# A graph layer on one core: GpSimd's order in the table stage, the last norm's square root and the width of the last down products

## The chip, the cores and the metric

The kernel runs on one core of one Trainium2 chip. The metric is the device time of one launch in microseconds (us); the time of a kernel is the median of its runs. The parts of the core are called PE (TensorE, the matmuls; PEld are its weight loads), DVE (VectorE), ACT (ScalarE), POOL (GpSimd) and SP (SyncE, which here only issues DMAs).

## The reference

625 nodes with 512 features, 20,625 edges sorted by destination (each with a source, one of four types and a weight). The layer is a normalized graph convolution, a feed-forward part and two more norms:

```python
h = relu(layernorm(x))
for r in range(4):
    msg += (h[src] @ W_rel[r] + b_rel[r]) * where(edge_type == r, edge_weight, 0)[:, None]
agg = segment_sum(msg, dst) / max(segment_sum(edge_weight, dst), 1)[:, None]
x1 = layernorm(h + h @ W_self + b_self + agg) * ln1_g + ln1_b
ffn = gelu(x1 @ W_ffn1 + b_ffn1) @ W_ffn2 + b_ffn2
out = x + layernorm(x1 + ffn) * ln2_g + ln2_b
```

W_rel and W_self are 512x512, W_ffn1 is 512x1024, W_ffn2 1024x512. All is float32.

## The kernel before, in words

The nodes lie in five blocks of 128 rows (the last has 113), the edges in 162 tiles of 128.

**Table stage** (lines 511 to 565, to about 116 us). For each of the four types r and each block i, `table_rows` (L218) multiplies the block of h by W_rel[r], adds the bias row and stores the 128x512 result into a table in DRAM, 20 blocks in all. In the first round each block's h must be made first: `variance` (L164) takes mean and variance on DVE, `pre_norm` (L207) takes 1/sqrt on POOL as a power of -0.5 (`rsqrt_pow`, L188), forms the bias nb on DVE (L210) and applies norm and relu on ACT (L211); `transposed` (L196) turns the block on PE and copies it with ACT into hT (L201). The turn of block i + 1 is written between the two halves of block i's four products (`between`, L221), and `next_norm(i + 2)` behind it. PE also adds up the edges of the first and last node block by one-hot products (`outer_hots`, `outer_sums`), which take key columns from `outer_columns` (L297).

`set_limits` (L258) fills `lim`, two rows of 162 numbers on each partition, by one POOL memset for each stretch of equal values (66 for the lower limits, 65 for the upper). The call for the lower ones is written after `next_norm(1)`, that for the upper ones at the end of the first round of r. The lower ones are read in `outer_columns` (L307), and both in `count_outside` (L268).

The order on an engine is the order written in the program for the engines that are named in `manual_schedule` (L511: PE, DVE, ACT). POOL isn't named, and there a scheduler chooses the order: all 131 memsets stand between the power of block 0 and that of block 1. SP issues the loads, the stores of the table and the later weights in order; the first twelve loads wait for nothing, later weights are issued between table stores.

**Edge stage** (L568 on). Tiles of edges are gathered from the table by indirect DMAs on POOL (L579), weighted on ACT and DVE and added up on PE by one-hot matmuls. A planner with written costs (`offer`, `run`, L616 on) puts the other work of PE between them: self products, products of the outer blocks, and for each block that is complete `norm_and_feed` (L631).

**The tail of a block**: `first_norm` (L449), a turn, and `feed_forward` (L461): eight steps `up` (four 128x128 products each, then a gelu on ACT into gT) and four steps `down` (two 128x512 products each). The last `down` step goes on: it adds the residual (L481), takes the statistics (L482), subtracts the mean and multiplies by g2 (L484, `ya`), takes 1/sqrt and forms the output (L486), and `store_block` (L491) issues the store. For four of the blocks 1/sqrt is made on DVE by `rsqrt_scaled` (L176: a shift and an integer step for the first guess, then three Newton steps of two operations, the result scaled by -8192; g1 and g2 are divided by that beforehand). The last block to be fed (`last`, L633) uses `rsqrt_pow` on POOL, a power and a multiplication, in both norms.

Behind this stands a branch (L696) that isn't taken with these inputs.

Of the kernel before, what the change touches and what calls it, by code (L numbers as in the profile page):

```python
# [9 lines left out]
F32 = mybir.dt.float32  # L10
F32R = mybir.dt.float32r
I32 = mybir.dt.int32
BF16 = mybir.dt.bfloat16
AF = mybir.ActivationFunctionType
ALU = mybir.AluOpType

P = 128
# [25 lines left out]
def gnn_layer(ctx, tc, x, edges, w_self, w_rel, w_ffn1, w_ffn2, rows_in, bf1_in, out, n_edges):  # L43
# [27 lines left out]
    HOTS = 4  # L71
# [92 lines left out]
    def variance(in_, name):  # L164

        st = work.tile([P, 6], F32, tag="bn", name=f"st_{name}")
        nc.vector.bn_stats(st, in_)
        mv = work.tile([P, 2], F32, tag="mv", name=f"mv_{name}", bufs=HOTS)
        nc.vector.bn_aggr(mv, st)
        t = work.tile([P, 3], F32, tag="rs", name=f"rs_{name}", bufs=HOTS)  # L170
        nc.vector.tensor_scalar(t[:, 0:1], mv[:, 1:2], EPS, None, op0=ALU.add)
        return mv[:, 0:1], t
# [124 lines left out]
    def outer_columns():  # L297


        ki = early.tile([P, 2, NE], I32, name="ki")  # L300
        nc.vector.tensor_copy(fl, ed[:, 0:3, :])
        k = 0
        for b, j0, n in outer:
            to, at = slice(k, k + n), slice(j0, j0 + n)
            nc.vector.tensor_scalar(ki[:, 0, to], ed[:, 0, at], P - 1, None, op0=ALU.bitwise_and)
            nc.vector.tensor_scalar(ki[:, 1, to], ed[:, 0, at], 7, None, op0=ALU.logical_shift_right)
            nc.vector.tensor_scalar(key[:, 2, to], lim[:, 0, at], float(b * P), None, op0=ALU.max)  # L307
            nc.vector.tensor_sub(key[:, 2, to], dst_f[:, at], key[:, 2, to])
            nc.vector.tensor_copy(w2[:, 0, to], wgt[:, at])
            nc.vector.tensor_sub(w2[:, 1, to], wgt[:, at], w2[:, 0, to].bitcast(F32))  # L310
            k += n
        nc.vector.tensor_copy(key[:, 0:2, :], ki)
        k = 0
        for _, j0, n in outer:
            to, at = slice(k, k + n), slice(j0, j0 + n)
            nc.vector.scalar_tensor_tensor(key[:, 1, to], typ_f[:, at], float(NB), key[:, 1, to],
                                           op0=ALU.mult, op1=ALU.add)
            k += n
        nc.vector.scalar_tensor_tensor(key[:, 1, :], key[:, 2, :], float(NC), key[:, 1, :],
                                       op0=ALU.mult, op1=ALU.add)  # L320
# [137 lines left out]
        return x1  # L458


    def feed_forward(x1T_b, gT, zi, xi, store, name, pool_pow=False, nn=P):  # L461
        po = []

        def up(f):
            pu = ps.tile([P, D], F32, tag="ps", name=f"pu_{name}_{f}")
            for k in range(KD):
                nc.tensor.matmul(pu[:, :nn], w1_sb[:, k, f * P:(f + 1) * P], x1T_b[:, k, :nn],  # L467
                                 start=(k == 0), stop=(k == KD - 1))
            nc.scalar.activation(gT[:, f, :nn], pu[:, :nn], AF.Gelu, bias=bf1[:, f:f + 1])

        def down(f):
            if f == 0:
                po.append(ps.tile([P, D], F32, tag="ps", name=f"po_{name}"))
            for f_ in (f, f + 1):
                nc.tensor.matmul(po[0][:nn], gT[:, f_, :nn], w2_sb[:, f_, :], start=(f_ == 0), stop=(f_ == KF - 1))  # L475
            if f + 2 < KF:
                return
            y = work.tile([P, D], F32, tag="ow", name=f"y_{name}", bufs=HOTS)
            if nn < P:
                nc.vector.tensor_copy(y, zi)  # L480
            nc.vector.tensor_add(y[:nn], po[0][:nn], zi[:nn])  # L481
            mean, t = variance(y, f"y{name}")  # L482
            a = work.tile([P, D], F32, tag="ow", name=f"ya_{name}", bufs=HOTS)
            nc.vector.scalar_tensor_tensor(a, y, mean, g2_bc, op0=ALU.subtract, op1=ALU.mult)  # L484
            rstd = rsqrt_pow(t, True) if pool_pow else rsqrt_scaled(t)
            nc.vector.scalar_tensor_tensor(y, a, rstd, xi, op0=ALU.mult, op1=ALU.add)  # L486
            store(y)

        return [lambda f=f: up(f) for f in range(KF)] + [lambda f=f: down(f) for f in range(0, KF, 2)]

    def store_block(b, o):  # L491
        n = min(P, N - b * P)
        whole = n if n == P else n // 16 * 16
        nc.sync.dma_start(out[b * P:b * P + whole, :], o[:whole])
        if whole < n:
            nc.scalar.dma_start(out[b * P + whole:N, :], o[whole:n])


    DG = 27
# [8 lines left out]
    for _, _, n in outer:  # L508
        groups += [(k + a, min(2, n - a)) for a in range(0, n, 2)]
        k += n  # L510
    with tc.manual_schedule(engines={PE, DVE, ACT}):  # L511
        stats = variance(xs[:, 0, :], "x0")

        def next_norm(i):
            nonlocal stats
            if i < NB:
                pre_norm(i, *stats)
            if i + 1 < NB:
                stats = variance(xs[:, i + 1, :], f"x{i + 1}")

        warm = ps_one.tile([P, D], F32, tag="one", name="warm")
        for _ in range(WARM):
            nc.tensor.matmul(warm, zeros[:, :P], zeros, start=True, stop=True)
        next_norm(0)
        hots, hots_1, made = [], [], 0
        pdeg = ps_one.tile([P, D], F32, tag="one", name="pdeg")
        transposed(hT, z[:, 0, :], 0, "h0")
        next_norm(1)
        set_limits(0)
        for r in range(R):  # L530
            for i in range(NB):
                def next_transposed():
                    transposed(hT, z[:, i + 1, :], i + 1, f"h{i + 1}")
                    next_norm(i + 2)

                table_rows(r, i, next_transposed if r == 0 and i + 1 < NB else None)
                while hots_1:
                    outer_sums(*hots_1.pop(0))
                if (r, i) == (0, 2):
                    outer_columns()  # L540
                for _ in range(2):
                    if (r, i) >= (0, 2) and groups:
                        hots_1.append(outer_hots(*groups.pop(0)))
                if (r, i) == (0, NB - 1):
                    set_limits(1)
                if (r, i) == (1, 0):
                    nc.scalar.activation(gelu_of, ones, AF.Gelu)
                    edge_columns()
                    cols = degree_columns()
                if r == 1:  # L550
                    nc.vector.tensor_add(z[:, i, :], z[:, i, :], bself_bc)
                    nc.vector.tensor_add(xs[:, i, :], xs[:, i, :], b2_bc)
                if (r, i) == (2, 0):
                    for g_bc in (g1_bc, g2_bc):
                        nc.vector.tensor_scalar(g_bc, g_bc, 1.0 / RS, None, op0=ALU.mult)
                if len(hots) > HOTS - 1 and (r, i) > (3, 0):
                    degree_sums(pdeg, *hots.pop(0))
                if r >= 2 and i > 0 and made < len(chunks):
                    hots.append(degree_hots(*chunks[made], *cols))
                    made += 1  # L560
                if (r, i) == (1, NB - 1):
                    total_outside = count_outside()
            later_loads(r)
        for made_ in hots_1:
            outer_sums(*made_)
    early_stack.close()
    edge = ctx.enter_context(tc.tile_pool(name="edge", bufs=3))
    with tc.manual_schedule(engines={PE}):  # L568
# [62 lines left out]
        def norm_and_feed(b):  # L631
            nonlocal ready
            last = b == inner[-1]  # L633
            need_self(b)
            x1 = first_norm(z[:, b, :], acc[b], rdeg[:, b:b + 1], b, pool_pow=last)
            ready = max(ready, now + NORM)
            ff = feed_forward(x1T[:, :, b * P:(b + 1) * P], gT, z[:, b, :], xs[:, b, :],
                              lambda o: store_block(b, o), b, pool_pow=last, nn=min(P, N - b * P))
            work_ = [(0.9, 1.0 if f == KF - 1 else 0.0, st) for f, st in enumerate(ff[:KF])]
            work_ += [(1.72, 0.0, st) for st in ff[KF:]]  # L640
            work_.append((0.0, 0.0, feed_next))

            def turned():
                transposed(x1T, x1, b, f"x1_{b}")
                to_feed.append(work_)
                if len(to_feed) == 1:
                    offer(10, now + 1.9, work_)

            offer(9, now + (9.0 if last else 15.0), [(0.7, 0.0, turned)])
# [46 lines left out]
    with tc.If(ends["outside"] > 0):  # L696
# [26 lines left out]
        with tc.For_i(0, NB, 1) as b:  # L723
# [11 lines left out]
            transposed(x1T, x1, 0, "x1_again")  # L735
            gT = const.tile([P, KF, P], F32, tag="gT", name="gT_again")
            for step in feed_forward(x1T[:, :, :P], gT, zb, xb,
                                     lambda o: nc.sync.dma_start(out[bass.ds(b * NG, NG), :], o[:NG]), "again"):
                step()


# [39 lines left out]
```

## Time and profile before

| | us |
|---|---|
| three runs | 322.49, 322.87, 326.82 |
| median | 322.87 |
| profiled execution, its time | 321.32 |
| its span | 319.6 |
| PE busy | 297.4 (93%) |
| DVE busy | 223.4 (70%) |
| ACT busy | 148.6 (46%) |
| POOL busy | 121.8 (38%) |

The span is what lies between the first and the last record of the execution; the rest of its time lies around it. Most of POOL's busy time (110.0 us) is the issue of 105 indirect DMAs. In the timeline a line gives the start, the duration, the engine, the line of the program, the operation and its tiles, and in brackets how long the engine was idle before, and what ended that. In the waits, a line gives who waited for whom, the sum, the number of times and the longest. DMA lines give the issuing queue, how many, the size of one, and the median time from issue to landing in us.

### The profile page before, as it was taken

Reading aid. Unit: us, or ns where it says so; the run is one execution under the profiler, and the core shown is the slowest. Engines: PE = TensorE matmul, PEld = TensorE weight load, DVE = VectorE, ACT = ScalarE, POOL = GpSimd, SP = SyncE. Lnnn points to the kernel's source line nnn. Section 1 sums busy time; section 2 is a strip of 40 time slices with the busy share of each in tenths; the row PEclk is TensorE's granted clock in tenths of the full one; section 3 lists DMA queues with packets and bytes.
Section 4 is the critical chain, followed back from the end, with each engine's and each line's share of the span. In section 5 each row is a group of like instructions: output and inputs, shape, how many; then the busy total and the mean of one; then the engine's idle time right before and its main releaser. Section 6 shows DMA issues by size and latency. Waiting matters only on the chain.

```text
span 319.6 us, 4430 instructions
## 1 busy us (share of the span) xinstructions
PE 297.4 (93%) x1360; PEld 187.5 (59%) x1361; DVE 223.4 (70%) x499; ACT 148.6 (46%) x313; POOL 121.8 (38%) x257
## 2 busy tenths in 40 slices
PE   7799999999999999999999999989999999999900
PEld 3344656665656675455456546865885975958500
DVE  3535698769999854666667999676999786965030
ACT  3236666455445634454465303676564655613100
POOL 7400000000000027777777703777774777310010
PEclk9999999999999999999999999999999999999985
DMA  7999911510011137868888823677773777500000
GB/s 242 369 403 386 371 47 66 165 66 33 34 68 51 49 106 224 261 183 256 299 297 284 252 77 101 175 215 203 206 208 115 199 204 205 151 29 33 5 35 0
DMA packets 20557, 53.33 MB, mean 167 GB/s; under 512 B 2817, under 2 KB 2817, under 8 KB 20402
## 3 DMA queue, kind: packets, MB, share of 16 engines
q0 software_dynamic: 8400, 27.53, 29.3%
q1 hardware_dynamic: 12128, 25.47, 21.9%
q8 instruction: 12, 0.20, 0.2%
q14 instruction: 15, 0.12, 0.1%
q10 hardware_dynamic: 2, 0.00, 0.0%
HBM read 45.16 MB, written 7.83 MB: 166 GB/s over the span
## 4 chain that ended last, share of the span: by engine, by line
PE 81%; DMA 4%; DVE 4%; POOL 3%; issue 3%; ACT 2%; POOLq 0%; ACTq 0%
PE pt L223 20%; PE po L475 11%; PE pu L467 9%; PE acc L441 9%; PE bank L357 8%; PE acc L603 7%; PE acc L602 7%; PE pz L238 5%; DMA ms<-table,row_i 3%; PE pdeg L402 2%; POOL lim L262 1%; POOL ms L579 1%; DVE lo L586 1%; DMA xs<-in_x_dram 1%; ACT ohw L334 1%
## 5 line engine op out<-in xcount | busy, mean ns | idle before, releaser
L579 POOL DMA_INDIRECT ms<-table,row_i x105 | 110.0, 1047 | 149.0 <-ACT sums_w L362 101.6
L584 ACT ACTIVATE hi<-ms,ed 128x512 fp32r<-128x512 f32 x105 | 74.8, 722 | 76.9 <-DMA ms<-table,row_i 37.0
L586 DVE SCALAR_TENSOR_TENSOR lo<-ms,ed,hi 128x512 fp32r<-128x512 f32 x105 | 77.8, 748 | 34.3 <-ACT hi L584 29.7
L223 PE MATMUL pt<-wr,hT 128*128 128x512 f32 x160 | 73.1, 598 | 0.8 <-ACT hT L201 0.7
L602 PE MATMUL acc<-hi,oh 128*128 128x512 f32 x117 | 61.4, 525 | 0.0
L334 ACT ACTIVATE ohw<-os,w 128x128 fp32r<-128x128 f32 x138 | 42.2, 389 | 23.5 <-DVE os L328 23.5
L603 PE MATMUL acc<-lo,oh 128*128 128x512 f32 x117 | 47.0, 402 | 1.5 <-DVE lo L586 1.4
L223 PEld LDWEIGHTS pt<-wr,hT 128*128 128x128 f32 x160 | 28.9, 190 | 29.6 <-issue 28.2
L467 PEld LDWEIGHTS pu<-x1T,w_sb 128*128 128x128 f32 x320 | 40.3, 191 | 3.3 <-ACT x1T L201 1.1
L467 PE MATMUL pu<-x1T,w_sb 128*128 128x128 f32 (+1 forms) x320 | 40.8, 275 | 0.7 <-ACT x1T L201 0.7
L357 PE MATMUL bank<-od,ohw 128*128 128x60 f32 (+18 forms) x216 | 40.0, 326 | 0.4 <-ACT ohw L334 0.4
L357 PEld LDWEIGHTS bank<-od,ohw 128*128 128x128 f32 x216 | 31.2, 191 | 10.8 <-issue 4.6
L475 PE MATMUL po<-w_sb,gT 128*128 128x512 f32 (+1 forms) x80 | 36.6, 592 | 0.0
L603 PEld LDWEIGHTS acc<-lo,oh 128*128 128x128 f32 x117 | 22.1, 189 | 14.4 <-DVE lo L586 6.4
L230 DVE TENSOR_TENSOR m<-pt,brel_bc 128x512 f32<-128x512 f32 x20 | 13.8, 688 | 21.5 <-PE pt L223 21.5
L441 PE MATMUL acc<-tr,sums_w 128*128 128x512 f32 x60 | 28.0, 595 | 0.3 <-DMA tr<-table 0.2
L602 PEld LDWEIGHTS acc<-hi,oh 128*128 128x128 f32 x117 | 22.2, 189 | 10.4 <-issue 5.5
L337 DVE TENSOR_SCALAR od<-key_row,key 128x320 fp32r<-128x320 f32 (+15 forms) x69 | 22.9, 374 | 0.0
L475 PEld LDWEIGHTS po<-w_sb,gT 128*128 128x128 f32 (+1 forms) x80 | 14.8, 187 | 13.6 <-issue 12.1
L598 DVE TENSOR_TENSOR oh<-fl,node_row 128x512 fp32r<-128x512 f32 (+1 forms) x30 | 19.9, 674 | 1.6 <-PE bank L357 1.6
L362 ACT COPY sums_w<-bank 128x500 f32<-128x500 f32 (+1 forms) x12 | 10.6, 919 | 20.3 <-PE bank L357 20.3
L238 PE MATMUL pz<-ws_sb,hT 128*128 128x512 f32 x40 | 17.6, 595 | 0.0
(107 smaller groups left out, 215.2 us busy)
## 6 DMA issues: line engine op xcount, KB each, us to landing
table<-m SPq DMA_DIRECT2D x20, 256.0 KB, 2.0
w_sb<-in_L_gnn_W_ffn_dram SPq DMA_DIRECT2D x2, 2048.0 KB, 10.6
tr<-table SPq DMA_DIRECT2D x15, 256.0 KB, 4.0
wr<-in_L_gnn_W_rel_dram SPq DMA_DIRECT2D x3, 1024.0 KB, 7.8
ms<-table,row_i POOLq DMA_INDIRECT x105, 3.8
rows<-in_rows_dram SPq DMA_DIRECT2D x1, 1536.0 KB, 14.8
z_kept<-z SPq DMA_DIRECT2D x5, 256.0 KB, 2.0
ws_sb<-in_L_gnn_W_self_dram SPq DMA_DIRECT2D x1, 1024.0 KB, 9.5
```

The costliest lines, as they stand in the source:

```text
L223: nc.tensor.matmul(p, hT[:, k, i * P:(i + 1) * P], wr_sb[r][:, k, :], start=(k == 0), stop=(k == KD - 1))
L238: nc.tensor.matmul(p, hT[:, k, i * P:(i + 1) * P], ws_sb[:, k, :], start=(k == 0), stop=(k == KD - 1))
L334: nc.scalar.activation(ohw[:, k - k0, part, :], oh[:, k - k0, :], AF.Copy, scale=w2[:, part, k:k + 1].bitcast(F32))
L357: nc.tensor.matmul(bank[q][:, (a - q * BW) * NC:(z_ - q * BW) * NC], ohw[:, k - k0, part, :], ow[:, (a - lo) * NC:(z_ - lo) * NC], start=F ...
L441: nc.tensor.matmul(acc[b], sums_w[b][:, order[i], :], kept[order[i]], start=(i == 0), stop=(i == NC - 1))
L467: nc.tensor.matmul(pu[:, :nn], w1_sb[:, k, f * P:(f + 1) * P], x1T_b[:, k, :nn], start=(k == 0), stop=(k == KD - 1))
L475: nc.tensor.matmul(po[0][:nn], gT[:, f_, :nn], w2_sb[:, f_, :], start=(f_ == 0), stop=(f_ == KF - 1))
L579: nc.gpsimd.indirect_dma_start(out=ms, out_offset=None, in_=table[:, :], in_offset=bass.IndirectOffsetOnAxis(ap=row_i[:, j:j + 1], axis=0))
L584: nc.scalar.activation(hi, ms, AF.Copy, scale=w)
L586: nc.vector.scalar_tensor_tensor(lo, ms, w, hi.bitcast(F32), op0=ALU.mult, op1=ALU.subtract)
L602: nc.tensor.matmul(acc[b], oh, hi, start=first, stop=False)
L603: nc.tensor.matmul(acc[b], oh, lo, start=False, stop=end)
```

## The change

1. POOL is added to the engines whose order is the written one in the table stage. By the built program POOL then has: power of block 0, power of block 1, the 66 memsets of the lower limits, the powers of blocks 2, 3 and 4, the 65 memsets of the upper limits, then the gathers. Nothing else moves on any engine in that stage.
2. The last block's second norm takes `rsqrt_scaled` on DVE in place of `rsqrt_pow` on POOL. Its first norm keeps the power.
3. The last block's down products are made in two halves of 256 columns, each with all eight steps of gT and its own PSUM tile; addition and statistics follow each half, and the two sets of statistics are aggregated together. Four closures as before, of four products each, so the planner sees the same list. The last operation and the store are made in two halves too.
4. The integer key columns are written into the float tile `key` itself and converted in place, and the tile `ki` goes.

```diff
-        ki = early.tile([P, 2, NE], I32, name="ki")
+        ki = key[:, 0:2, :].bitcast(I32)
...
-            mean, t = variance(y, f"y{name}")
+            st = work.tile([P, 6], F32, tag="bn", name=f"st_y{name}")
+            nc.vector.bn_stats(st, y)
+            second_norm(y, st)
+
+        def second_norm(y, st):
+            mean, t = aggregate(st, f"y{name}")
             a = work.tile([P, D], F32, tag="ow", name=f"ya_{name}", bufs=HOTS)
             nc.vector.scalar_tensor_tensor(a, y, mean, g2_bc, op0=ALU.subtract, op1=ALU.mult)
-            rstd = rsqrt_pow(t, True) if pool_pow else rsqrt_scaled(t)
-            nc.vector.scalar_tensor_tensor(y, a, rstd, xi, op0=ALU.mult, op1=ALU.add)
-            store(y)
+            rstd = rsqrt_scaled(t)
+            for c in (slice(0, H), slice(H, D)) if halves else (slice(0, D),):
+                nc.vector.scalar_tensor_tensor(y[:, c], a[:, c], rstd, xi[:, c], op0=ALU.mult, op1=ALU.add)
+                store(y, c)
+
+        y_st = []
+
+        def down_half(h, f):
+            c = slice(h * H, (h + 1) * H)
+            if f == 0:
+                po.append(ps.tile([P, D], F32, tag="ps", name=f"po_{name}_{h}"))
+            for f_ in range(f, f + 4):
+                nc.tensor.matmul(po[h][:, :H], gT[:, f_, :], w2_sb[:, f_, c], start=(f_ == 0), stop=(f_ == KF - 1))
+            if f + 4 < KF:
+                return
+            if h == 0:
+                y_st.append(work.tile([P, D], F32, tag="ow", name=f"y_{name}", bufs=HOTS))
+                y_st.append(work.tile([P, 2, 6], F32, tag="bn", name=f"st_y{name}"))
+            y, st = y_st
+            nc.vector.tensor_add(y[:, c], po[h][:, :H], zi[:, c])
+            nc.vector.bn_stats(st[:, h, :], y[:, c])
+            if h == 1:
+                second_norm(y, st)
...
+            downs = [lambda h=h, f=f: down_half(h, f) for h in range(2) for f in range(0, KF, 4)]
...
-    with tc.manual_schedule(engines={PE, DVE, ACT}):
+    with tc.manual_schedule(engines={PE, DVE, ACT, mybir.EngineType.Pool}):
...
-                              lambda o: store_block(b, o), b, pool_pow=last, nn=min(P, N - b * P))
+                              lambda o, c: store_block(b, o, c), b, halves=last, nn=min(P, N - b * P))
```

`aggregate` is the second half of `variance`: it aggregates the statistics and adds the epsilon. H is 256, D 512, KF 8.

More of the change, by code (lines that the diff above doesn't have):

```diff
@@ L167, in variance, with aggregate @@
         nc.vector.bn_stats(st, in_)
+        return aggregate(st, name)
+    def aggregate(st, name):
         mv = work.tile([P, 2], F32, tag="mv", name=f"mv_{name}", bufs=HOTS)
@@ L458, in first_norm, with feed_forward @@
         return x1
-    def feed_forward(x1T_b, gT, zi, xi, store, name, pool_pow=False, nn=P):
+    def feed_forward(x1T_b, gT, zi, xi, store, name, halves=False, nn=P):
         po = []
+        H = D // 2
         def up(f):
@@ L486, in down @@
-            nc.vector.scalar_tensor_tensor(y, a, rstd, xi, op0=ALU.mult, op1=ALU.add)
-            store(y)
-        return [lambda f=f: up(f) for f in range(KF)] + [lambda f=f: down(f) for f in range(0, KF, 2)]
-    def store_block(b, o):
+            rstd = rsqrt_scaled(t)
[3 more added lines that the diff above has]
+        y_st = []
@@ L492, in store_block @@
+        if halves:
+            downs = [lambda h=h, f=f: down_half(h, f) for h in range(2) for f in range(0, KF, 4)]
+        else:
+            downs = [lambda f=f: down(f) for f in range(0, KF, 2)]
+        return [lambda f=f: up(f) for f in range(KF)] + downs
+    def store_block(b, o, c):
         n = min(P, N - b * P)
         whole = n if n == P else n // 16 * 16
-        nc.sync.dma_start(out[b * P:b * P + whole, :], o[:whole])
+        nc.sync.dma_start(out[b * P:b * P + whole, c], o[:whole, c])
@@ L495, in store_block @@
         if whole < n:
-            nc.scalar.dma_start(out[b * P + whole:N, :], o[whole:n])
+            nc.scalar.dma_start(out[b * P + whole:N, c], o[whole:n, c])
     DG = 27
@@ L737, in gnn_layer @@
             for step in feed_forward(x1T[:, :, :P], gT, zb, xb,
-                                     lambda o: nc.sync.dma_start(out[bass.ds(b * NG, NG), :], o[:NG]), "again"):
+                                     lambda o, c: nc.sync.dma_start(out[bass.ds(b * NG, NG), :], o[:NG]), "again"):
                 step()
```

## The prediction

> **What bounds the kernel now.** I read the page's slices first, then PE's waits, then the timelines of the two places that the change touches, and the transfers of the start.
>
> The page says which engine to follow: PE is busy in nine tenths of nearly every slice, at the full granted clock, and carries 81% of the chain of work that ended last.
>
> ```profile
> PE   7799999999999999999999999989999999999900
> ...
> PEclk9999999999999999999999999999999999999985
> ...
> PE 81%; DMA 4%; DVE 4%; POOL 3%; issue 3%; ACT 2%; POOLq 0%; ACTq 0%
> ```
>
> So a gain needs a place where PE stands still, or the end, where PE is done. PE's waits in the first 120 us name the first place:
>
> ```profile
> PE tp_h L200 <- ACT z L211: 1.7, 1, 1.7
> ...
> PE pt L223 <- ACT hT L201: 0.7, 1, 0.7
> ...
> PE bank L357 <- ACT ohw L334: 0.4, 1, 0.4
> ```
>
> The timeline shows where the 1.7 us come from: the variance of block 1 is there at 6.43 (6.28 + 0.15), but its power on POOL starts at 9.62, behind 131 memsets, and nb, z and PE's transposes follow it one by one.
>
> ```profile
> 4.63 0.55 POOL L191 TENSOR_TENSOR rs_x<-rs_x,half 128x1 f32<-128x1 f32 x1 [1.66 <-DVE rs_x L171]
> ...
> 5.13 4.53 POOL L262 MEMSET lim<- 128x1 f32 x131
> ...
> 6.28 0.15 DVE L171 TENSOR_SCALAR rs_x<-mv_x 128x1 f32<-128x1 f32 x1
> ...
> 7.66 1.98 PE L223 MATMUL pt<-wr,hT 128*128 128x512 f32 x4 [0.68 <-ACT hT L201]
> ...
> 9.62 0.55 POOL L191 TENSOR_TENSOR rs_x<-rs_x,half 128x1 f32<-128x1 f32 x1
> ...
> 10.21 0.21 DVE L210 TENSOR_SCALAR nb<-mv_x,rs_x 128x1 f32<-128x1 f32 x1 [3.77 <-POOL rs_x L191]
> ...
> 11.32 0.66 PE L200 MATMUL tp_h<-ident,z 128*128 128x128 f32 x4 [1.68 <-ACT z L211]
> ```
>
> The other place is the end: the last down product, then a serial line of DVE and POOL, then one store.
>
> ```profile
> 304.10 0.69 DVE L481 TENSOR_TENSOR y<-po,z 128x512 f32<-128x512 f32 x1 [10.50 <-PE po L475]
> ...
> 304.83 0.69 DVE L167 BATCH_NORM_STATS2 st_y<-y 128x6 f32<-128x512 f32 x1
> ...
> 305.77 0.15 DVE L171 TENSOR_SCALAR rs_y<-mv_y 128x1 f32<-128x1 f32 x1
> ...
> 306.01 0.99 POOL L191 TENSOR_TENSOR rs_y<-rs_y,half 128x1 f32<-128x1 f32 x1 [20.91 <-DVE rs_y L171]
> ...
> 307.30 0.75 DVE L486 SCALAR_TENSOR_TENSOR y<-ya,rs_y,xs 128x512 f32<-128x512 f32 x1 [0.71 <-POOL rs_y L193]
> ...
> 308.08 0.33 SPq L494 DMA_DIRECT2D out_dram<-y  x1
> ```
>
> **The start, part by part.** The built order of the changed kernel differs on POOL only here: power 0, power 1, then the 66 memsets of the lower limits, powers 2, 3, 4, then the 65 of the upper ones. One memset takes 4.48 us / 131 = 34 ns in the chain, so 66 take 2.26 us.
> - Block 1: power at 6.5, ready at 7.06; nb until 7.3; ACT is in the copy of hT until 7.61, then z takes 0.81: 8.43. The first two products of pt (four instructions of 0.43 from 7.66, plus 0.22, which is the 0.66 of a transpose group that waited less the 0.44 of one that didn't) end at 9.60. So z is 1.2 us early and PE goes straight on: transposes done at 9.60 + 0.44 = 10.04, before at 11.98. That is **1.94 us** (the wait of 1.68 and a refill of 0.26); from 1.68, the wait alone, to 2.16, if the refill after 7.66 is no part of it.
> - What is late next: block 2's power now stands behind the 66 memsets: 7.06 + 2.26 = 9.3, power 9.9, nb 10.1, z 11.3 (behind hT of block 1 on ACT). PE wants it after 10.04 + 3.43 = 13.5: 2.2 us to spare. nb of block 2 holds DVE from 8.3 to 9.9; queued behind it are block 3's statistics and the first table addition, which has its product only at 11.8.
> - Transfers stay where they are, because SP issues the first twelve without any wait. They become the next limit:
>
> ```profile
> rows<-in_rows_dram SPq DMA_DIRECT2D x1, 1536.0 KB, 14.8
> ...
> wr<-in_L_gnn_W_rel_dram SPq DMA_DIRECT2D x1, 512.0 KB, 5.3
> xs<-in_x_dram SPq DMA_DIRECT2D x1, 512.0 KB, 7.3
> ...
> brel_bc<-in_rows_dram SPq DMA_DIRECT2D x1, 256.0 KB, 6.4
> ```
>
>  With their issues at 6.26, 3.07, 4.06 and 3.55, the rest of the first weights lands at 8.4 (wanted at 10.04), the bias rows at 9.95 (wanted at 11.8), blocks 3 and 4 of x at 11.4. Those last ones make block 3's statistics wait on DVE from 10.1 to 11.4 and push the first table addition to about 12.5, its row store to 13.2 (before 14.45); block 3's z is then ready about 15.3, wanted at 17.3. The table stores and later weights move up by 1 to 2 us on SP, but queue in order behind the 1.5 MB of rows that land at 21.1 as before; the fourth table addition, which reuses the first one's buffer, comes at about 24.4. Slack 3 us.
> - After block 2 PE is released by its own earlier products through DVE and ACT (key columns, hot rows); these move up with it, so the 1.94 us reach the end. The upper limits are read only near 62 us.
> - The key columns converted in place: same number of instructions. In place or not, rows agree (z<-z at L551 683 ns, z<-x at L457 684), so nothing, 0.1 either way at most; behind it stand the hot rows that PE waits 0.4 for.
>
> **The end, part by part**, against PE's last product ending at 304.08:
> - 16 products of 512 columns (6.88 us, 0.43 each) become 32 of 256. Eight of 128 columns take 0.89 in the chain, 0.111 each: 0.84 ns a column at 512, 0.87 at 128. Between them 0.215 to 0.222: 6.88 to 7.11. I take **+0.1** (0 to 0.23). A gain would need a column cheaper than in either row.
> - Addition and statistics of the first half lie beside the second half's products (DVE is idle there for 10.5 us). Of the second half, a 256-wide pass instead of a 512-wide one: 0.42 (os, L328) against 0.69, twice: **-0.54**. Aggregating two sets instead of one: nothing, 0.05 at most.
> - Power and scaling on POOL go, eight small DVE steps come, in line behind ya. The previous block shows this very sequence: variance at 290.38 to last operation at 292.85, 2.47 us. Before, 305.77 to 307.30, 1.53. **+0.94**; this is no estimate by size, so 0.9 to 1.0. POOL is left with nothing after the first norm, which no one waits for.
> - Last operation in two halves: 0.75 - 0.27 = 0.48 each, the second starting about 0.08 before the first ends (the key columns at L305 and L306 do so): the second ends at 0.88. **+0.13** (0 to 0.2).
> - The store: 256 KB took 2.8 us to land, of which the DMA rate stands above 240 GB/s for 0.8. The last half moves 128 KB: **-0.4** (-0.8, if its data hide wholly behind the first; +0.3, if its issue waits out the first's 0.33 on SP and lands no sooner).
> - Sum of the end: 0.1 - 0.54 + 0.94 + 0.13 - 0.4 = **+0.23** (-0.4 to +1.2). What follows the landing (310.9 to 319.6) has no work of the program and stays.
>
> Weighed against this: the Trainium skill, TensorE: Matmul & The Clock Gate, section Back-to-back issue gap, gives sustained spacings of 81 ns at 128 columns and 131 at 512, so that narrow products cost more per column. By an estimate from these two, 256 columns would cost about 98/131 of the wide one, two halves 1.5 times, +3.4 us instead of +0.1, and the sum of all would be +1.6, slower. This trace has 0.111 against 0.43, in proportion to the columns, so I stay with the rows.
>
> **Sum.** -1.94 + 0.23 = -1.7 us. The profiled execution took 321.32 (span 319.6): it would take 319.6 (span 317.9). The median of the three runs, 322.87, lies 1.55 above the profiled execution; taken from it, the time is 321.2.
>
> **Rivals.**
> 1. The start's gain is eaten by transfers: the rest of the first weights, or the table stores, are late, and PE waits elsewhere before 34 us (DMA is at its full share from 8 to 34 us). For it: that share. Against: each landing above has 1.5 us or more to spare. Then only the end's +0.23 stays: 323.1; in part, 322.
> 2. Slower: the narrow last products don't cost by columns, since each half loads all its weights again. At 0.43 for any width it would be +6.9, net +5.1: 328.0. From 0.27 each (+1.8) it decides against the gain. Against: 64 products of 128 columns just ahead, each with its own weights, run at 0.111.
> 3. The end gets shorter, not longer: the store's data hide wholly and the second operation costs nothing more, end -0.4: 322.87 - 1.94 - 0.4 = 320.5.
> 4. The change doesn't do what it says: the order on POOL stays. The built order speaks against it; I give it nothing.
>
> **How the numbers follow.** Forecast 0.68 with its own range 320.3 to 322.4 (ends of the terms: -2.16 - 0.4 and -1.68 + 1.2); rival 1 0.14, rival 2 0.06, rival 3 0.12. 321.2 is the forecast's. The runs shown spread by more than the change: the profiled execution is 1.55 below the median. So the range goes to 319.4 below and 323.4 above, which takes in rival 1 and leaves out rival 2 and outer drift. About 2% (6.5 us) is what a measurement of this kernel can tell from no change; no case but rival 2 at its worst comes near. Faster by over 2%: 0.02, within: 0.95, slower: 0.03.
>
> **What would show it.** In the changed profile: one power on POOL near 6.5, no wait of PE's transposes on z after the first block, the first product group after them at about 10.0; PE's last work about 1.8 earlier than 304.08; products of 256 columns at 0.22 apart; 2.4 to 2.5 us from the last variance to the last operation; the last landing about 2.4 us after its issue. A new wait of PE before 34 us, above all on wr or on DVE's m, would make the prediction wrong, and so would spacings over 0.27 at the end.

## The result, and the profile after

| | before | after |
|---|---|---|
| median of four runs each, us | 322.68 | 314.44 |
| their span of values | 321.98 to 326.82 | 314.11 to 314.95 |
| profiled execution | 321.32 | 314.15 |
| its span | 319.6 | 312.4 |
| first products of block 1's turn (tp_h) begin at | 11.32 | 9.57 |
| first self product (pz) begins at | 119.10 | 117.33 |
| PE's last product ends at | 304.06 | 303.42 |
| last operation of DVE ends at | 308.05 | 307.95 |
| last byte of the output lands at | 310.84 | 310.58 |
| from PE's last product to the end of the span | 15.49 | 8.96 |

By the medians the changed kernel is 8.2 us faster, where 1.7 was predicted; the ratio is 0.9755, with a 95% interval of 0.9733 to 0.9776. Some executions of a kernel are slower than the rest (326.82 is one): the ratios and intervals in this document leave them out, the medians don't. The two profiled executions differ by 7.2; the other 1.1 is how far each lies below its own median (1.36 before, 0.29 after).

The table already says where to look. Up to the last landing the two executions differ by 0.26 us, which is less than predicted. The other 6.9 lie behind the landing, where the program has no work.

**The start.** The timeline of the changed kernel, at the places shown of before:

```profile
6.82 0.15 DVE L174 TENSOR_SCALAR rs_x<-mv_x 128x1 f32<-128x1 f32 x1
7.05 0.55 POOL L194 TENSOR_TENSOR rs_x<-rs_x,half 128x1 f32<-128x1 f32 x1 [1.78 <-DVE rs_x L174]
...
7.54 2.32 POOL L265 MEMSET lim<- 128x1 f32 x66
7.64 0.21 DVE L213 TENSOR_SCALAR nb<-mv_x,rs_x 128x1 f32<-128x1 f32 x1 [0.67 <-POOL rs_x L194]
7.75 1.98 PE L226 MATMUL pt<-wr,hT 128*128 128x512 f32 x4 [0.68 <-ACT hT L204]
...
9.57 0.60 PE L203 MATMUL tp_h<-ident,z 128*128 128x128 f32 x4
...
12.07 0.69 DVE L167 BATCH_NORM_STATS2 st_x<-xs 128x6 f32<-128x512 f32 x1 [1.45 <-DMA xs<-in_x_dram]
```

The power of block 1 (7.05) now stands ahead of the 66 memsets (7.54), and PE's turn at 9.57 has no bracket: it waited for nothing. PE's waits of the first 120 us agree:

```profile
PE warm L557 <- DVE rs_col L158: 1.2, 1, 1.2
PE tp_h L203 <- ACT z L214: 0.9, 1, 0.9
PE pt L226 <- ACT hT L204: 0.7, 1, 0.7
PE bank L360 <- ACT ohw L337: 0.2, 1, 0.2
```

The wait of 1.7 on z is gone. The 0.9 that is left stands ahead of block 0's turn: there the warm-up products ended at 5.48 instead of 6.26, while the turn itself starts at 6.42 for 6.33. Block 1's turn ends at 10.17 instead of 11.98, and from the products behind it on, all in the table stage is 1.77 to 1.81 earlier.

**The edge stage** gives some of it back: from the first self product to the last turn it takes 170.50 us instead of 169.40. The chain of waits between 115 and 290 us (after) has more of the gathers in it:

```profile
by line: DMA ms<-table,row_i 20.9%; issue 16.9%; PE acc L444 11.9%; PE pz L241 9.9%; POOL ms L613 9.9%; DVE lo L620 5.7%; PE acc L637 4.5%; PE acc L636 4.4%; ACT hi L618 4.2%; PE po L480 3.9%; PE pu L472 2.2%; PE pdeg L405 1.4%; DVE oh L632
```

Before, over the same stretch, the gathers' transfers had 5.3% and their issue on POOL 2.1%:

```profile
by line: PE acc L441 16.8%; PE po L475 15.7%; PE acc L603 13.3%; PE pu L467 12.9%; PE acc L602 12.7%; PE pz L238 9.9%; DMA ms<-table,row_i 5.3%; issue 4.5%; POOL ms L579 2.1%; DVE lo L586 1.7%; PE pdeg L402 1.4%; ACT hi L584 0.8%; ACT sums_
```

By POOL's timeline the first gather is issued 1.79 earlier than before (116.08 for 117.87), the last only 0.29 earlier (273.98 for 274.27), and the 105 issues took 112.6 us instead of 110.0. So the gathers lose the gain on the way, and a chain that runs through them with it. Why their issues were longer, no run here settles, nor that the order on POOL is behind it: in the runs further down with gathers they took 110.6 to 112.8 us with the order and 110.1 to 114.0 without. With the last block as long as before within 0.04, 0.64 of the 1.77 us is left at PE's last product.

**The end.** The timeline of the changed kernel, with POOL's last two operations on top:

```profile
283.13 1.00 POOL L194 TENSOR_TENSOR rs_z<-rs_z,half 128x1 f32<-128x1 f32 x1 [8.21 <-DVE rs_z L174]
...
284.22 0.19 POOL L196 TENSOR_TENSOR rs_z<-rs_z,rs_col 128x1 f32<-128x1 f32 x1
...
303.46 0.42 DVE L514 TENSOR_TENSOR y<-po,z 128x256 f32<-128x256 f32 x1 [2.57 <-PE po L507]
303.92 0.43 DVE L515 BATCH_NORM_STATS2 st_y<-y 128x6 f32<-128x256 f32 x1
...
304.62 0.15 DVE L174 TENSOR_SCALAR rs_y<-mv_y 128x1 f32<-128x1 f32 x1
...
307.07 0.88 DVE L497 SCALAR_TENSOR_TENSOR y<-ya,rs_y,xs 128x256 f32<-128x256 f32 x2
307.58 0.81 SPq L528 DMA_DIRECT2D out_dram<-y  x2
```

Two half-wide passes of 0.42 and 0.43, 2.45 from the variance to the last operation, 0.88 for that in halves: DVE's path is as long as predicted. What differs is POOL. Its last operation ends at 284.41, where before it ended at 307.26. Behind a program's last operation each engine still has a closing sequence, which the listing of a program line's instructions shows (after the operation: how many, minimum, median and maximum of one in ns, first and last start in us; a q behind the engine's name marks its sequencer). Before, the branch behind the blocks (L696) and the end of the program (L777):

```profile
L696 POOLq INC_SWDGE_SEM  x1: 2267/2267/2267, 307.8 to 307.8; - x1
```

```profile
L777 SPq EVENT_SEMAPHORE  x14: 17/28/958, 308.9 to 319.5; - x14
...
L777 POOLq DRAIN  x3: 40/107/8640, 310.1 to 319.3; - x3
...
L777 PEldq DRAIN  x2: 8/8/8, 304.3 to 319.1; - x2
```

After, the same two places (now L730 and L811):

```profile
L730 POOLq INC_SWDGE_SEM  x1: 2267/2267/2267, 284.9 to 284.9; - x1
```

```profile
L811 SPq EVENT_SEMAPHORE  x14: 17/28/28, 308.9 to 312.3; - x14
...
L811 POOLq DRAIN  x3: 40/107/8640, 287.2 to 312.1; - x3
```

The instructions are the same and take the same time: INC_SWDGE_SEM 2.27 us, then a DRAIN of 8.64. Only their place differs. Before, they follow an operation that ends at 307.26: INC from 307.79 to 310.06, DRAIN from 310.10 to 318.74, the last exchange of semaphores, end of the span at 319.55. That is 12.29 us from POOL's last operation, and the landing at 310.84 lies in the middle of it. After, the long DRAIN ends at 295.87, beside the last block's products. SP's waits at the end show the change too. Before:

```profile
SPq L777 <- PEq L777: 8.4, 2, 7.9
...
SPq L777 <- DMA ms<-table,row_i: 1.0, 1, 1.0
...
SPq L777 <- DMA out_dram<-y: 0.3, 1, 0.3
```

After:

```profile
SPq L811 <- DMA out_dram<-y: 1.5, 1, 1.5
...
SPq L811 <- PEq L811: 0.7, 2, 0.5
```

Before, SP had the output after 0.3 us and then stood 7.9 us in the last barrier of all engines. The line blames PEq, but PE's sequencer had made its first closing DRAIN at 304.3; POOL arrived last. After, SP waits for the store, and 0.5 us in the barrier.

### The profile page after: what moved, and what is told of

The parts are those of the page before. It is cut to its first block, busy times and chain, and to the rows that moved or that the text cites. A ratio compares the mean times of both kernels' runs of the same rounds, so it can differ in the third digit from the quotient of the medians.

```text
span 312.4 us, 4472 instructions
## 1 busy us (share of the span) xinstructions
PE 297.7 (95%) x1377; PEld 190.0 (61%) x1377; DVE 225.6 (72%) x510; ACT 148.3 (47%) x313; POOL 123.4 (40%) x255
## 4 chain that ended last, share of the span: by engine, by line
PE 58%; DMA 13%; issue 10%; DVE 8%; POOL 6%; ACT 4%; ACTq 0%; POOLq 0%; DVEq 0%
PE pt L226 21%; DMA ms<-table,row_i 12%; PE bank L360 8%; PE acc L444 7%; PE pz L241 6%; POOL ms L613 6%; PE pu L472 3%; DVE lo L620 3%; PE acc L637 3%; PE acc L636 2%; ACT hi L618 2%; PE po L507 2%; PE po L480 2%; PE pdeg L405 2%; DMA xs<-in_x_dram 1%
## 5 line engine op out<-in xcount | busy, mean ns | idle before, releaser
L613 POOL DMA_INDIRECT ms<-table,row_i x105 | 112.6, 1073 | 144.3 <-ACT sums_w L365 98.1
L480 PE MATMUL po<-w_sb,gT 128*128 128x512 f32 (+1 forms) x64 | 29.6, 592 | 0.0
L480 PEld LDWEIGHTS po<-w_sb,gT 128*128 128x128 f32 (+1 forms) x64 | 11.8, 186 | 10.2 <-issue 8.7
```

Source lines behind the costliest of these rows:

```text
L613: nc.gpsimd.indirect_dma_start(out=ms, out_offset=None, in_=table[:, :], in_offset=bass.IndirectOffsetOnAxis(ap=row_i[:, j:j + 1], axis=0))
```

## The experiments

The theory: the gain is POOL's closing sequence. The square root on POOL kept it from starting until 3.2 us after PE's last product; without it, it runs beside the last block. Rival A: the gain is that of the order on POOL in the table stage, more than the profile's shift shows. Rival B: it is that of the two halves, through a shorter store and end.

On the chips of the experiments the granted clock was 0.96 to 0.99, and the kernel before took 337 to 341 us, with 1.5 to 2.4% between its fastest and slowest run. The medians and ratios below are against the kernel before on the same chip. Medians therefore settle effects of several us only. The smaller ones are read from two distances inside the profile, which the earlier stages don't touch: from PE's last product to the end of the span, and from POOL's last operation to it.

### One part alone

The order alone, on the kernel before:

```diff
-    with tc.manual_schedule(engines={PE, DVE, ACT}):
+    with tc.manual_schedule(engines={PE, DVE, ACT, mybir.EngineType.Pool}):
```

> Only POOL's written order in the table stage; the end is as before. Theory (the 7 us come from the end of the program: POOL's closing drain of 8.64 us now lies beside other work): the end keeps its length, so only the start's 1.8 us can show, less up to 1.1 that the edge stage gave back in the changed profile: 0.7 to 1.8 us faster than before. Rival A (the order in the table stage carries the gain, by way of the later stages): 6 us or more faster.

The Newton steps alone, on the kernel before:

```diff
-            rstd = rsqrt_pow(t, True) if pool_pow else rsqrt_scaled(t)
+            rstd = rsqrt_scaled(t)
```

> Only the last norm's square root on DVE. Theory: POOL has its last work some 22 us earlier, its drain is hidden, and the data path gets 0.94 us longer: last operation at about 309.0, landing 311.8, span about 312.8, that is 6.5 to 7 us faster than before. Prediction on record: the data path alone counts, 0.9 us slower. Rival A: no gain.

The halves alone (with the in-place key columns), against the changed kernel:

```diff
-            rstd = rsqrt_scaled(t)
+            rstd = rsqrt_pow(t, True) if halves else rsqrt_scaled(t)
...
-    with tc.manual_schedule(engines={PE, DVE, ACT, mybir.EngineType.Pool}):
+    with tc.manual_schedule(engines={PE, DVE, ACT}):
```

> Only the halves; the power stays on POOL, the table stage's order is the scheduler's. Theory: POOL's last work comes 0.5 us earlier (two 512-wide passes become 256-wide behind PE's last product), and the end follows it by the same 12.3 us: 0.3 to 0.6 us faster than before. Rival B (the halves, with their earlier stores, carry the gain): 5 us or more faster.

The changed kernel with the power back, that is, order and halves without Newton:

```diff
-            rstd = rsqrt_scaled(t)
+            rstd = rsqrt_pow(t, True) if halves else rsqrt_scaled(t)
```

> The changed kernel with the last norm's power put back on POOL; order and halves stay. Theory: the drain is exposed again: start 0.7 to 1.8 and halves 0.5 faster than before, 320.4 to 321.5, 6 us or more slower than the changed kernel. Rivals A and B: about the changed kernel's 314.4.

All on one chip; the last two columns are in us.

| | median / before | ratio, 95% | PE's last product to end | POOL's last operation to end |
|---|---|---|---|---|
| before (its profile above) | | | 15.49 | 12.29 |
| changed (its profile above) | | | 8.96 | 27.97 |
| order alone | 337.20 / 337.72 | 0.9956 (0.9906 to 1.0007) | 15.49 | 12.30 |
| Newton alone | 331.14 / 337.72 | 0.9742 (0.9669 to 0.9816) | 9.11 | 28.1 |
| halves alone | 337.83 / 337.72 | 0.9999 (0.9957 to 1.0041) | 14.99 | 12.30 |
| order and halves | 334.31 / 337.72 | 0.9875 (0.9795 to 0.9955) | 14.99 | 12.29 |

The one line of Newton steps makes 6.6 us by the medians, 6.2 to 11.2 by the interval and 6.38 by the end of the profile. The order alone and the halves alone leave the time where it was within their intervals, and both rivals fall as explanations of the 6.9. Order and halves together came out 1.5 to 6.9 us faster by the interval, where 1.2 to 2.3 were expected; at the end of the profile they make the 0.50 of the halves alone. In the kernel before and the three others with the power on POOL, the span ends 12.29 to 12.30 after POOL's last operation, to a hundredth. With Newton alone, the end of the program reads as in the changed kernel, DRAIN first started early:

```profile
L777 POOLq DRAIN  x3: 40/107/8640, 305.0 to 330.0; - x3
```

and SP's waits are again on the store:

```profile
SPq L777 <- DMA out_dram<-y: 1.7, 1, 1.7
...
SPq L777 <- PEq L777: 0.7, 2, 0.5
```

With the power back in the changed kernel, the DRAIN starts at 322.4, 4 us after the power (318.28), and all waits for it:

```profile
L811 POOLq DRAIN  x3: 40/107/8640, 322.4 to 331.6; - x3
```

### One part undone

The changed kernel without the order, and without the halves:

```diff
-    with tc.manual_schedule(engines={PE, DVE, ACT, mybir.EngineType.Pool}):
+    with tc.manual_schedule(engines={PE, DVE, ACT}):
```

> The changed kernel with the table stage's POOL order left to the scheduler again. Theory: it loses what the start's 1.8 us are worth at the end: 315.1 to 316.2 (0.7 to 1.8 slower than the changed kernel). If the edge stage swallows the start's gain, 314.4 to 314.9. Rival A: 320 or more.

```diff
-                              lambda o, c: store_block(b, o, c), b, halves=last, nn=min(P, N - b * P))
+                              lambda o, c: store_block(b, o, c), b, halves=False, nn=min(P, N - b * P))
```

> The changed kernel with whole down products, one addition, one last operation and one store in the last block. Theory: last operation ends about 0.4 us later (1.69 + 2.47 + 0.75 = 4.91 after PE's end against 4.52), the one store lands 2.8 after its issue against 2.6: 0.3 to 0.8 slower than the changed kernel, 314.7 to 315.2. Rival B (the halves carry the gain): 319 or more.

Without the order: 335.44 against 341.22, ratio 0.9798 (0.9734 to 0.9862), 9.00 from PE's last product to the end. Without the halves: 332.35, ratio 0.977 (0.9705 to 0.9836), 8.98. Each keeps the large gain, as it should if neither made it.

The halves are worth 0.50 while POOL's power is in the way (15.49 against 14.99), since POOL's last operation then comes 0.5 earlier. Once it isn't, they are worth nothing that shows: 8.98 without, 8.96 with. DVE's last operation does end 0.38 earlier with them (4.53 instead of 4.91 after PE's last product), but from the issue of the last store to the end it takes 4.37 instead of 4.04. SP closes the program by looking at its semaphores one after another, mostly 0.06 to 0.09 us apart. With two stores the semaphore of the last is early in that list: its landing is seen at 310.60, seven checks stand behind it, one of them 0.41 after the one before, and SP is done at 311.58. With one store it is last in the list, and SP is done 0.13 after it (327.58 after 327.45). That the place in the list is what eats the 0.38 is read from these rows; another order of it wasn't tried, and what the step of 0.41 is, they don't say.

### A needless operation on POOL

If the closing sequence is the cause, an operation whose result nobody reads must bring the old time back, and by an amount set by where it ends. The first is put behind the last block's aggregation, where the power stood, the second behind the statistics of its first half:

```diff
+            if halves:
+                idle = work.tile([P, 1], F32, tag="idle", name="idle", bufs=1)
+                nc.gpsimd.tensor_tensor(idle, t[:, 0:1], rs_col, op=ALU.mult)
```

> The changed kernel with one more POOL operation of one column (128x1, product never used) behind the last norm's variance, off the data path. Theory: POOL's last work then ends at about 305.05 of the changed profile, and the end follows 12.3 us behind: 317.3 against 312.4 of span, 4.9 us slower, about 319.3. Prediction on record and rivals A and B: nothing, 314.4.

```diff
+            if h == 0:
+                idle = work.tile([P, 1], F32, tag="idle", name="idle", bufs=1)
+                nc.gpsimd.tensor_tensor(idle, st[:, 0, 0:1], rs_col, op=ALU.mult)
```

> The same unused POOL operation behind the first half's statistics, 3.9 us earlier. Theory: last POOL work ends at about 301.1, end 12.3 behind: 313.4 of span, 1.0 us slower than the changed kernel, about 315.4. Prediction on record and rivals A and B: nothing, 314.4.

The late one, by its timeline and the listing of the program's end:

```profile
320.14 0.63 POOL L495 TENSOR_TENSOR idle<-rs_y,rs_col 128x1 f32<-128x1 f32 x1 [20.45 <-DVE rs_y L174]
```

```profile
L814 POOLq DRAIN  x3: 40/107/8640, 323.2 to 332.4; - x3
```

The early one:

```profile
321.42 0.19 POOL L518 TENSOR_TENSOR idle<-st_y,rs_col 128x1 f32<-128x1 f32 x1 [16.57 <-DVE st_y L515]
```

```profile
L814 POOLq DRAIN  x3: 40/107/8640, 324.5 to 333.6; - x3
```

The late one ends 2.06 us after PE's last product, and the span ends 11.86 after it: 13.92 from PE's last product, 4.96 more than in the changed kernel, at 4.9 expected. (11.86 and not 12.30 because the branch behind it follows 0.4 sooner here.) The early one ends 2.26 before PE's last product; 12.30 later is 10.04, which is 1.08 more than the changed kernel at 1.0 expected. The medians are 336.53 and 332.35 against 341.22, ratios 0.9889 (0.9811 to 0.9968) and 0.9726 (0.9655 to 0.9798). So a multiplication of one column, off every chain of data, costs 5 us at the end where it comes late, and 1.1 where it comes 4.3 us earlier. By these, POOL's last operation has to end 12.30 - 8.96 = 3.3 us before PE's last product to be hidden in this kernel.

### What the closing sequence waits for

The gathers are replaced by plain loads of table rows issued by SP, so that POOL issues no DMA at all (other rows are gathered and the sums differ, and the span of the whole isn't compared):

```diff
-            nc.gpsimd.indirect_dma_start(
-                out=ms, out_offset=None, in_=table[:, :],
-                in_offset=bass.IndirectOffsetOnAxis(ap=row_i[:, j:j + 1], axis=0))
+            nc.sync.dma_start(ms, table[j % NC * P:(j % NC + 1) * P, :])
```

> The changed kernel with each gather on POOL replaced by a plain load of 128 table rows in order, issued by SP (the rows are not those of the edges). It asks what POOL's closing drain belongs to; its time is not to be compared. Theory: the drain closes POOL's own DMA issues, and is far shorter than 8.64 us when the program has issued none. Rival: it is a fixed price of the program's end, 8.64 us again.

The listing of the branch, then of the end of the program:

```profile
L728 POOLq INC_SWDGE_SEM  x1: 163/163/163, 281.9 to 281.9; - x1
```

```profile
L809 POOLq DRAIN  x3: 40/50/93, 282.1 to 308.5; - x3
```

INC_SWDGE_SEM takes 0.16 instead of 2.27 us, and no DRAIN there is longer than 0.093. So some 10.7 of the 12.3 us are the price of closing a POOL that has issued DMAs itself. The two instructions took 2.27 to 2.28 and 8.64 in all the other kernels above, whether they began 10 us after the issue of the last gather (the changed kernel: 274.93, 284.9) or 33 us (before: 275.2, 307.8). The last gather had landed at 277.7 and 277.8, so they don't wait for transfers under way. Whether the price depends on the number of gathers (105 here) wasn't tried.

### Fewer Newton steps, and the start once more

With POOL out of the way, DVE's path sets the end. Two steps instead of three, with another first guess:

```diff
-            rstd = rsqrt_scaled(t)
+            rstd = rsqrt_two(t) if halves else rsqrt_scaled(t)
```

```python
    def rsqrt_two(t):
        v, y, a = (t[:, j:j + 1] for j in range(3))
        nc.vector.tensor_scalar(y.bitcast(I32), v.bitcast(I32), 1, None, op0=ALU.logical_shift_right)
        nc.vector.tensor_scalar(y.bitcast(I32), y.bitcast(I32), -1.0, float(0x5FB759DF - (1 << 31)),
                                op0=ALU.mult, op1=ALU.add)
        for three in (12.0, 768.0):
            nc.vector.scalar_tensor_tensor(a, y, v, y, op0=ALU.mult, op1=ALU.mult)
            nc.vector.scalar_tensor_tensor(y, a, three, y, op0=ALU.subtract, op1=ALU.mult)
        return y
```

> The changed kernel with two Newton steps in place of three in the last block's second norm (the first guess takes sign and scale, so that the product is -8192 / sqrt as before, less exactly). Theory: the data path sets the end now, since the drain is hidden: two operations fewer, 0.22 + 0.16 + 0.07 between them, the end is 0.45 us nearer to PE's last product: 8.5 against 8.96 us. If anything on POOL still set the end, no change.

The timeline of its end:

```profile
320.03 0.15 DVE L174 TENSOR_SCALAR rs_y<-mv_y 128x1 f32<-128x1 f32 x1
...
322.02 0.88 DVE L508 SCALAR_TENSOR_TENSOR y<-ya,rs_y,xs 128x256 f32<-128x256 f32 x2
```

1.99 from the variance to the last operation instead of 2.45, and 8.51 from PE's last product to the end instead of 8.96, where 8.5 was expected (with three steps on the same chip, in the two runs below, 9.04 and 9.02). That the whole 0.45 arrives shows that DVE's path is the bound there now. In the median it is too small to see: 329.45 against 337.07, ratio 0.9801 (0.9745 to 0.9858).

On the same chip, the changed kernel as it is, and without the order a second time, to size the start:

> The changed kernel again, on the chip of the next run, for the start's share. Theory: 6.5 to 8.5 us faster than before.

> The changed kernel with the table stage's POOL order left to the scheduler, on the chip of the run before. Theory: PE stands 1.7 us for the first block's z again, and 0.7 to 1.8 us of it are left at the end: slower than the changed kernel by that. If the edge stage swallows it: the same within 0.3.

330.93 and 329.82 against 337.07, ratios 0.9781 (0.9719 to 0.9843) and 0.9803 (0.9739 to 0.9868). The intervals overlap almost wholly: by the medians the start's share can't be told from zero or from 2 us. In the profiles the turn of block 1 begins at 9.4 to 9.9 with the order and at 11.3 to 11.4 without, always. The first self product comes at 117.3 to 117.5 with the order and at 119.1 to 119.4 without, when the granted clock is full in the first 40 us. In five of nine profiles with the order the clock sank (0.81 from 24 to 33 us), which cost some 1.9, and in one of five without. Whether the earlier start brings that about, or chance, stays open.

## Why the prediction was wrong

**The step that failed** is the last sentence on the end: "What follows the landing (310.9 to 319.6) has no work of the program and stays." The first half is true, the second doesn't follow. Those 8.7 us were not a constant of the launch. They were the rest of a sequence that began when POOL finished, 12.29 us before the end. So the remark "POOL is left with nothing after the first norm, which no one waits for" put at nothing what decided: at the end all engines wait for each other (in the listing of L777, ACT, PE and DVE make their first closing DRAIN at 298.4, 304.3 and 308.6 and their next at 319.0 to 319.1), so all were waiting for POOL. The missing term is 1.80 - 8.71 = -6.91 from the landing to the end of the span. With it, PE's last product to the end goes from 15.49 to 8.96, -6.53, where the sum had +0.23 (0.13 of it behind that product). The rows were there: the listing of L777 and L696 of the kernel before, shown above, has the DRAIN of 8640 ns and its start at 310.1, and SP's wait of 7.9 us stands between the landing and the end.

The Trainium skill, VectorE: DVE Perf Modes, section The DRAIN you can't avoid, gives the runtime's own DRAINs about 12 ns, constant and on all five engines. Those of the listings above stand at a line of the program (L777, L811), and POOL's longest takes 8640 ns after gathers and 93 without, so that figure is no guide to them.

**The start**: -1.94 predicted; -1.81 measured at the first product group, -1.77 at the first self product. The mechanism was right: the power stands ahead of the memsets, z is early, PE goes straight on. The transfers moved a little, which the forecast did not foresee. The same rows of the changed kernel's transfers:

```profile
rows<-in_rows_dram SPq DMA_DIRECT2D x1, 1536.0 KB, 14.9
...
wr<-in_L_gnn_W_rel_dram SPq DMA_DIRECT2D x1, 512.0 KB, 5.9
xs<-in_x_dram SPq DMA_DIRECT2D x1, 512.0 KB, 8.0
...
brel_bc<-in_rows_dram SPq DMA_DIRECT2D x1, 256.0 KB, 7.1
```

The last three landed 0.6 to 0.7 later after their issues than before, still ahead of PE's need. Block 1's power ran at 7.05 and not at 6.5 because its rows of x came late in this execution (DVE waited 0.35 for them); z had 1.2 us to spare by the forecast and absorbed it (it ended at 8.70, and the turn began at 9.57).

"These move up with it, so the 1.94 us reach the end" was wrong in size, in these two profiles: PE's last product is only 0.64 earlier. The steps named as released by PE's own earlier products did move. The gathers did not keep up, and the edge stage took 1.1 longer.

**The end up to the landing**, term by term:

| term | predicted | measured |
|---|---|---|
| 32 narrow products for 16 wide | +0.1 | +0.04 (6.92 for 6.88) |
| addition and statistics of half width | -0.54 | -0.53 (0.42 and 0.43 for 0.69 each) |
| Newton on DVE for the power on POOL | +0.94 | +0.92 (2.45 for 1.53) |
| last operation in halves | +0.13 | +0.13 (0.88 for 0.75) |
| store of the last half, issue to landing | -0.4 | -0.19 (2.57 for 2.76) |

Each lies within its bounds where bounds were given. Between the last product and the last landing it makes +0.38 (7.16 for 6.78), and predicted was +0.13 without the products: the store is the term that was mis-sized, and two sets instead of one in the aggregation, put at nothing, took 0.03 more (0.21 for 0.18).

On the products, the rule of the Trainium skill (TensorE: Matmul & The Clock Gate, section Back-to-back issue gap), by which the prediction's estimate was +3.4, doesn't hold for these float32 products: 256 columns took 0.216 us, half of the 0.43 of 512.

**The rivals.** Rival 2 (narrow products dear) didn't come, and the order on POOL did change, against rival 4. Rival 1 has a part of truth: two thirds of the start's gain were indeed lost before PE's last product, but in the edge stage, on a chain through the gathers, and not at the first transfers. Rival 3 said that the end gets shorter, and it got shorter by 6.53 instead of 0.4, by another cause. None of them looked past the landing. The range was built from the terms of the start and of the end up to the landing, and the case that decided wasn't among them.

## What to carry to other kernels

The end of a kernel is not the landing of its last store: list each engine's instructions behind its last operation, the sequencer's too, and ask which engine reaches the last barrier last. Here, where GpSimd had issued 105 gathers, the end came 12.3 us after its last operation or later (11.9 in one kernel), so the smallest operation on GpSimd in the last norm cost more than the same work done more slowly on another engine. When a wait at a barrier is put down to an engine that had long been done, look for the one that arrived last.

## What the runs showed of the hardware that was not expected

- Closing POOL cost 2.27 us (INC_SWDGE_SEM) and 8.64 us (DRAIN) in every kernel in which POOL had issued gathers, and 0.16 and at most 0.093 where it had issued none. The size is the same 10 and 33 us after the issue of the last gather.
- SP's closing checks of its semaphores run one after another, mostly 0.06 to 0.09 us apart, with one step of 0.41 in the changed kernel; the store whose semaphore stands early in that list took 0.33 us longer from its issue to the end (4.37 for 4.04).
- The granted clock sank (0.81 from 24 to 33 us) in some executions of both orders, at a price of about 1.9 us, as much as the whole gain at the start.
